# Two cross-attention layers on one core: layer 0's scores computed once and kept in SBUF, column maxima added back; turns of 128 queries, groups of four heads

## The chip, the core and the metric

One Trainium2 chip, of which the program uses one core. The metric is the time of one execution on the device in microseconds (us); the time before is 3849.66 us, the median of three runs (3845.82, 3850.59 and 3849.66). The profile is of one further execution, of 3851.3 us, whose instructions span 3849.6 us. Everything is float32.

## The reference: what is computed

Batch of 4, 512 queries of 320 channels, 1024 context rows of 512 channels, 20 heads of 16 channels. Two layers, one after the other, each with a residual:

```python
# layer 0 (x: 4 x 512 x 320, ctx: 4 x 1024 x 512; the last 4 context rows are "ip", the other 1020 "text")
probs_t  = softmax(q @ k_text.T * 0.25)              # per head: 512 x 1020
text_out = probs_t @ v_text                          # per head: 512 x 16
qsem     = l2norm(probs_t @ ctx_text)                # per head: 512 x 512, the costly product
fused    = q @ k_ip.T * 0.25 + 0.5 * qsem @ l2norm(ctx_ip).T
ip_out   = (softmax(fused) * spatial_mask) @ v_ip
x        = (text_out + ip_out) @ W_out + b_out + x
# layer 1 (the first 77 context rows are "text", the other 947 "ip")
x        = (softmax(q k_text) v_text + softmax(q k_ip) v_ip) @ Wo + bo + x
```

The product of every head's probabilities with the whole context (`qsem`) is needed only for its norm and its product with four vectors, but the norm needs all 512 channels, so each head multiplies 512 x 1020 by 1020 x 512.

## The kernel before

**Units of work.** A turn of layer 0 is a batch entry and a half `sh` of 256 queries; a group (`gi`, 80 in all) is one turn and a pair `p` of heads. A group has two `Head` units. A unit multiplies the exponentials `e` (in quarters: two 128-query halves by two halves of the context rows) by the context with a Strassen-like scheme of seven products (`part0` to `part3`, tiles `b`), each of four matmuls with 256 moving columns, or 277 where the 21 columns of this head's values (16 values, 4 products with the normalised ip rows, a one for the sum) are taken along through a window loaded by `window` (L709). POOL forms the sums of quarters (`sum2`, L754, L771, L774), DVE and ACT take the products out of PSUM, add and square them.

**Scores of layer 0, before: twice.** For each group and each `c` of four, `do_max` (L655) computes scores with queries on the partitions (`max_fill`, two matmuls of 512 columns, 16 rows deep, tile `mx`), and DVE takes the row maximum from PSUM (L663). `subtract_max` (L462) turns the maxima with two PE transposes (`pt_nm`) and puts them as extra rows under the queries (`qa`). `do_exp` (L671, `exp_fill` L448) computes the scores a second time with the context rows on the partitions (four matmuls of 256 columns, 19 rows deep, tile `ex`), so that the maximum is subtracted inside the matmul, and ACT exponentiates from PSUM into SBUF (L459). The 16 or 19 rows of a head lie in one of four 32-row groups of PE's array; a pair of heads uses two of them, and the next pair the other two.

**Layer 1** (`layer1_half`, L485) does the same, its scores twice, with two softmaxes over 77 and 947 rows, and multiplies by values 32 columns wide (`do_pv`, L520, tile `pv`, four heads in four 32-column groups). Its work lies in the queue `l1` and is taken out one step at a time.

**What sets the order.** PE executes in program order. Between the parts of a unit stand stops: `stop_a` (L924) takes one item from the queues (a moved maximum, a piece of the end of a turn, a step of the next batch entry's projections), then does `do_max` of group `gi + 2` and `do_exp` of `gi + 1`; `stop_b` (L939) takes an item and one step of layer 1. Other engines' instructions are placed by a scheduler near that order; each engine then runs its own list in order, and SP issues nearly all DMAs in its list's order. PSUM: two score tiles of two banks (`ps_sc`, tag `sc`), three banks for the products (`qs0` to `qs2`), one (`tp`) for everything else.

**Before and behind the loop.** Batch entry 0 is projected ahead of the loop, both layers' keys and values (L893 to L897), then the first two groups' scores. After the last group, layer 1 of the last 256 queries has nothing beside it.

In `queries` (L237) and the output projections (L566, L872) the 320 channels are contracted in chunks of 128, 128 and 64 rows.

Of the kernel before, what the change touches and what calls it, by code (L numbers as in the profile page):

```python
# [20 lines left out]
P = 128  # L21
# [3 lines left out]
NIP = 4  # L25
# [8 lines left out]
SH = S // 2  # L34
NP = H // 2
QT = 256


R_TXT, R_IP, R_ALL, KR = 16, 17, 18, 19
V0W = D + NIP + 1  # L40
# [6 lines left out]
NEVER = -1e30  # L47
ATTN_SCALE = 0.25
# [5 lines left out]
def xattn_pair(ctx_stack: ExitStack, tc: tile.TileContext, a: dict, out: bass.AP):  # L54
# [8 lines left out]
    ep = pool("ep", 8)  # L63
    st2 = pool("st2", 2)
# [13 lines left out]

    idle = [True]
# [23 lines left out]
    qq = [[cst.tile([P, SH], F32, name=f"qq{l}_{i}") for i in range(1 + l)] for l in range(2)]  # L103
    nmz = [[cst.tile([P, 2, P], F32, name=f"nmz{l}_{i}") for i in range(1 + l)] for l in range(2)]
# [6 lines left out]
    last = cst.tile([P, 2], F32, name="last")  # L111
    wq = [cst.tile([P, NC, C], F32, name=f"wq{i}") for i in range(2)]
# [9 lines left out]
    def load_x(b, sh, pl, tag):  # L122
        t = pl.tile([P, 2, C], F32, tag=tag, name=f"{tag}_{b}_{sh}")
        nc.sync.dma_start(t, a["x"][b, sh * SH : (sh + 1) * SH, :].rearrange("(t p) c -> p t c", p=P))
        return t
# [3 lines left out]
    def load_w(b, *names):  # L129
# [11 lines left out]
        if names == ("L0_xattn_W_v",):  # L141
# [4 lines left out]

    load_chunks(wq[0], "L0_xattn_W_q")
    nc.scalar.dma_start(bo[0], a["L0_xattn_b_out"].partition_broadcast(P))


    rows0 = st3.tile([2, T], F32, tag="e1", name="rows0")
    nc.gpsimd.memset(rows0, 1.0)
    nc.gpsimd.affine_select(out=rows0[:, 0:NTXT0], in_=rows0[:, 0:NTXT0], compare_op=ALU.not_equal, fill=0.0, base=-1,
                            pattern=[[0, NTXT0]], channel_multiplier=1)

    rows = st3.tile([3, T], F32, tag="e1", name="rows")
    nc.gpsimd.memset(rows, 1.0)
    nc.gpsimd.affine_select(out=rows[:, 0:NTXT1], in_=rows[:, 0:NTXT1], compare_op=ALU.not_equal, fill=0.0, base=-1,
                            pattern=[[0, NTXT1]], channel_multiplier=1)
    nc.gpsimd.affine_select(out=rows[:, NTXT1:T], in_=rows[:, NTXT1:T], compare_op=ALU.not_equal, fill=0.0, base=0,  # L160
                            pattern=[[0, T - NTXT1]], channel_multiplier=1)
    for l in range(2):
        for i in range(1 + l):
            nc.vector.memset(qq[l][i], 0.0)
            nc.vector.memset(nmz[l][i], 0.0)
            for r in range(4):
                if l:
                    nc.scalar.dma_start(kq[l][i][32 * r + R_TXT : 32 * r + KR, :], rows)
                else:
                    nc.scalar.dma_start(kq[l][i][32 * r + R_ALL : 32 * r + KR, :], rows0[0:1, :])  # L170
                    nc.scalar.dma_start(kq[l][i][32 * r + R_IP : 32 * r + R_ALL, :], rows0[1:2, :])
                    nc.scalar.dma_start(kq[l][i][32 * r + R_TXT : 32 * r + R_IP, :], rows0[1:2, :])
    nc.vector.memset(nmz[0][0].rearrange("p j (r n) -> p (j r) n", r=4)[:, :, R_IP], NEVER)
# [3 lines left out]
                            pattern=[[0, 2]], channel_multiplier=-1)  # L177
    for n in ("21", "t4"):
        nc.gpsimd.memset(xv[n], 0.0)
# [38 lines left out]
    def transposed_half(src, name, tag):  # L218

        t = big.tile([P, NC, SH], F32, tag=tag, name=name)  # L220

        def front():
            pt = tp(f"pt_{name}_a")
            for c in range(2):
                for j in range(2):
                    tr(pt[:, c * SH + j * P : c * SH + (j + 1) * P], src[:, j, c * P : (c + 1) * P], ident)
            evac(t[:, 0:2, :].rearrange("p c s -> p (c s)"), pt)

        def back():
            pt = tp(f"pt_{name}_b")  # L230
            for j in range(2):
                tr(pt[:64, j * P : (j + 1) * P], src[:, j, 2 * P : C], ident)
            evac(t[:64, 2, :], pt[:64, 0:SH])

        return t, [front, back]

    def queries(t, w, dst, name, tag):  # L237

        o = (st2 if tag == "kst" else big).tile([P, NC, SH], F32, tag=tag, name=f"qs_{name}")

        def front():
            pt = tp(f"pt_{name}_a")
            for c in range(2):
                for i, (_, n) in enumerate(CK):
                    mm(pt[:, c * SH : (c + 1) * SH], w[:n, i, c * P : (c + 1) * P], t[:n, i, :], i == 0, i == NC - 1)
            nc.vector.tensor_scalar(o[:, 0:2, :].rearrange("p c s -> p (c s)"), pt, ATTN_SCALE, None, ALU.mult)

        def back():
            pt = tp(f"pt_{name}_b")
            for i, (_, n) in enumerate(CK):  # L250
                mm(pt[:64, 0:SH], w[:n, i, 2 * P : C], t[:n, i, :], i == 0, i == NC - 1)
            nc.vector.tensor_scalar(o[:64, 2, :], pt[:64, 0:SH], ATTN_SCALE, None, ALU.mult)
            nc.sync.dma_start(dst[0 : 2 * P, :].rearrange("(c p) s -> p c s", p=P), o[:, 0:2, :])
            nc.sync.dma_start(dst[2 * P : C, :], o[:64, 2, :])

        return [front, back]

    def projections(b):
# [5 lines left out]
        z.qd = [[dr.tile([C, SH], F32, tag=f"q{l}_{sh}", name=f"qd{l}_{b}_{sh}") for sh in range(2)] for l in range(2)]  # L264
# [4 lines left out]
        def quarter(n):  # L269
# [4 lines left out]
            def buffer(tag, shape):  # L274

                return (big if b else ep).tile(shape, F32, tag=tag if b else "e0", name=f"{tag}_{b}_{n}")
# [118 lines left out]
            if n == 0:  # L395
                v1[0:1] = [lambda: values1_first(0), lambda: values1_first(1)]
            return [[lambda: turn(0), lambda: (turn(1), sums())], [lambda: keys(0)], [lambda: keys(1)], [last_keys],
                    [lambda: values0(0), lambda: values0(1)], v1, [values_ip] if n == 3 else []]

        quarters = [quarter(n) for n in range(4)]  # L400

        for kinds in quarters if b else zip(*quarters):
            for kind in kinds:
                steps += kind
        for sh in range(2):
            hold = {}

            def first(sh=sh, hold=hold):
                t, hold["x"] = transposed_half(load_x(b, sh, big, "xin"), f"xT0_{b}_{sh}", "raw")
                hold["q"] = queries(t, wq[0], z.qd[0][sh], f"q0_{b}_{sh}", "kst")  # L410
                hold["x"][0]()

            steps += [first, lambda hold=hold: hold["x"][1](), lambda hold=hold: hold["q"][0](),
                      lambda hold=hold: hold["q"][1]()]
        return z, steps


    def pair(p):
        return p // 2, 2 * (p % 2)

    def place(l, turn, p):


        g, r0 = pair(p)
        return buffer(l, turn, g), r0
# [4 lines left out]
    def load_pair(l, z, turn, g, i):  # L430
        k = buffer(l, turn, g)
        for r in range(2 * i, 2 * i + 2):
            c = 64 * g + 16 * r
            nc.sync.dma_start(qq[l][k][32 * r : 32 * r + D, :], z.qd[l][turn % 2][c : c + D, :])
            nc.sync.dma_start(kq[l][k][32 * r : 32 * r + D, :], z.kd[l][c : c + D, :])

    def max_fill(l, turn, p, c, name):

        k, r0 = place(l, turn, p)
        j, half = c // 2, c % 2  # L440
        ps = ps_sc.tile([P, 2, 512], F32, tag="sc", name=f"mx{name}_{c}")
        for i in range(2):
            r = 32 * (r0 + i)
            mm(ps[:, i, :], qq[l][k][r : r + D, j * P : (j + 1) * P],
               kq[l][k][r : r + D, half * 512 : half * 512 + 512], True, True)
        return ps

    def exp_fill(l, turn, p, c, qa, name):  # L448

        k, r0 = place(l, turn, p)  # L450
        ps = ps_sc.tile([P, 2, 512], F32, tag="sc", name=f"ex{name}_{c}")
        for j in range(2):
            for i in range(2):
                r = 32 * (r0 + i)
                t = (2 * c + j) * P
                mm(ps[:, i, j * SH : (j + 1) * SH], kq[l][k][r : r + KR, t : t + P], qa[r : r + KR, :], True, True)
        pl = st3 if l else ep
        e = pl.tile([P, 2, 2, SH], F32, tag=f"e{l}", name=f"e{name}_{c}")
        nc.scalar.activation(e.rearrange("p i j s -> p (i j s)"), ps.rearrange("p i n -> p (i n)"), AF.Exp)  # L459
        return e  # L460

    def subtract_max(l, turn, p, z, name):  # L462

        k, r0 = place(l, turn, p)
        pt = tp(f"pt_nm{name}")
        for j in range(2):
            tr(pt[:, j * P : (j + 1) * P], z[:, j, :], ident)
        lo = 32 * r0
# [4 lines left out]
    def nm_at(z, j, p, row):  # L473

        lo = 32 * (2 * (p % 2))
        return z[:, j, lo : lo + 64].rearrange("p (i n) -> p i n", i=2)[:, :, row]
# [537 lines left out]
```

## Time and profile before

| | |
|---|---|
| median of 3 runs | 3849.66 us |
| profiled execution | 3851.3 us (span 3849.6 us) |
| PE, matmuls | 3710.9 us busy, 96% of the span, 21972 records |
| PE, weight loads | 2633.4 us, 68% |
| DVE / ACT / POOL | 42% / 31% / 27% |
| first to last product `b` (the loop) | 196.1 to 3624.4 us |
| scores `ex` / `mx`, both layers | 759.0 us / 732.1 us of PE |
| DMA | 196.11 MB, most from SP's queue |

A line of the profile names the source line, the engine, the operation, the tile written and the tiles read with their shapes, and the number of records. A float32 matmul leaves two records, so that `ex ... x8` is four matmuls. "Busy" of PE is the union of records, whose ends are modelled: the distance between the starts of records says more than their lengths. The granted clock (PEclk) is 1.00 where PE has its full clock.

### The profile page before, as it was taken

How to read it: one execution, taken by the hardware profiler on the slowest of the kernel's cores; microseconds unless marked ns; L12 is line 12 of the kernel's file. 1: busy time of each engine (PE TensorE's matmuls, PEld its weight loads, DVE VectorE, ACT ScalarE, POOL GpSimd, SP SyncE). 2: the span in 40 equal slices, each digit the busy share in tenths (PEclk: the TensorE clock that was granted, in tenths of full speed). 3: DMA queues.
4: the chain of work that ended last, by engine and by line, in shares of the span. 5: the costliest groups of instructions: out<-in, count | busy, mean ns of one | idle time of the engine just before them, and what ended most of it. 6: DMA issues, size and time to landing. Idle time of an engine off the chain costs nothing.

```text
span 3849.6 us, 57354 instructions
## 1 busy us (share of the span) xinstructions
PE 3710.9 (96%) x21972; PEld 2633.4 (68%) x21972; DVE 1622.4 (42%) x3089; ACT 1195.9 (31%) x2424; POOL 1033.4 (27%) x1376
## 2 busy tenths in 40 slices
PE   5899999999999999999999999999999999999887
PEld 4577777677776777767776777767776676766533
DVE  1222234444434445344543545334544445355343
ACT  0122223233322333323332333323333333233222
POOL 1032233233322222223322222223332332322100
PEclk9899999999999999999999999999999999999955
DMA  6424411111232231211223232211211111111100
GB/s 178 121 67 109 108 41 17 18 28 23 59 74 64 66 89 37 53 37 28 67 52 76 62 74 48 53 34 28 61 22 31 29 22 26 30 21 25 24 19 13
DMA packets 541488, 196.11 MB, mean 51 GB/s; under 512 B 428056, under 2 KB 530936, under 8 KB 541216
## 3 DMA queue, kind: packets, MB, share of 16 engines
q1 hardware_dynamic: 540608, 192.10, 22.0%
q8 instruction: 175, 2.87, 0.3%
q14 instruction: 97, 0.79, 0.1%
q10 hardware_dynamic: 608, 0.35, 0.0%
HBM read 149.39 MB, written 40.16 MB: 49 GB/s over the span
## 4 chain that ended last, share of the span: by engine, by line
PE 91%; DVE 4%; DMA 3%; issue 1%; SPq 0%; ACT 0%; POOL 0%; POOLq 0%; DVEq 0%; ACTq 0%
PE b L74 53%; PE mx L74 11%; PE ex L74 9%; PE pv L74 5%; PE pt_k L74 4%; PE pt_v L74 4%; PE pt_y L74 2%; PE pt_q_a L74 1%; DVE den L550 1%; DVE m L506 1%; PE pt_nm L77 1%; DMA v1d<-v 1%; DMA raw<-in_ctx_dram 1%; PE pt_q_b L74 1%; DVE den L547 0%
## 5 line engine op out<-in xcount | busy, mean ns | idle before, releaser
L459 ACT ACTIVATE e<-ex 128x1024 f32<-128x1024 f32 x640 | 654.7, 1023 | 658.6 <-PE ex L74 655.6
L74 PE MATMUL ex<-qa,kq 19*128 19x256 f32 x5120 | 759.0, 417 | 10.1 <-DVE qa L517 7.3
L74 PE MATMUL mx<-kq,qq 16*128 16x512 f32 x2560 | 732.1, 673 | 28.1 <-DVE m L506 20.2
L74 PE MATMUL b<-xv_t,e 128*128 128x277 f32 x2560 | 674.2, 406 | 6.2 <-DVE c L762 6.0
L74 PE MATMUL b<-xv,e 128*128 128x277 f32 x2560 | 639.7, 402 | 0.5 <-DVE qa L470 0.5
L74 PEld LDWEIGHTS b<-xv_t,e 128*128 128x128 f32 x2560 | 471.5, 190 | 169.5 <-issue 54.0
L74 PEld LDWEIGHTS b<-xv,e 128*128 128x128 f32 x2560 | 473.8, 190 | 151.4 <-issue 44.8
L74 PEld LDWEIGHTS ex<-qa,kq 19*128 19x128 f32 x5120 | 454.9, 192 | 79.7 <-issue 16.7
L663 DVE TENSOR_REDUCE m<-mx 128x2 f32<-128x1024 f32 x320 | 390.0, 1219 | 222.5 <-PE ex L74 215.7
L758 ACT ACTIVATE junk<-c 128x256 f32<-128x256 f32 x480 | 200.2, 417 | 879.1 <-DVE c L762 879.0
L754 POOL TENSOR_TENSOR s<-e,e 128x256 f32<-128x256 f32 x320 | 228.6, 725 | 796.7 <-ACT e L459 648.3
L506 DVE TENSOR_REDUCE m<-mx 128x2 f32<-128x870 f32 (+1 forms) x320 | 364.4, 1139 | 170.1 <-PE ex L74 152.5
L675 POOL TENSOR_TENSOR e<-e 128x512 f32<-128x512 f32 x160 | 204.6, 1279 | 785.4 <-ACT e L459 776.7
L762 DVE TENSOR_TENSOR c<-b,p 128x256 f32<-128x256 f32 x320 | 134.1, 419 | 611.6 <-PE b L74 568.6
L74 PEld LDWEIGHTS mx<-kq,qq 16*128 16x128 f32 x2560 | 195.8, 191 | 246.6 <-issue 185.8
L74 PE MATMUL b<-xs,e 128*128 128x256 f32 x1280 | 318.6, 392 | 3.6 <-DVE p L782 3.6
L74 PE MATMUL b<-xs_t,e 128*128 128x256 f32 x1280 | 319.4, 392 | 1.4 <-POOL e L771 1.4
L771 POOL TENSOR_TENSOR e<-e,s 128x256 f32<-128x256 f32 x320 | 232.4, 728 | 325.9 <-PE b L74 325.9
L74 PE MATMUL b<-xs_t,s 128*128 128x256 f32 x1280 | 307.5, 383 | 0.0
L74 PEld LDWEIGHTS b<-xs,e 128*128 128x128 f32 x1280 | 233.5, 191 | 81.9 <-issue 41.6
L74 PEld LDWEIGHTS b<-xs_t,e 128*128 128x128 f32 x1280 | 229.9, 189 | 79.6 <-issue 26.2
L74 PEld LDWEIGHTS b<-xs_t,s 128*128 128x128 f32 x1280 | 241.7, 191 | 47.4 <-issue 15.6
(190 smaller groups left out, 2907.8 us busy)
## 6 DMA issues: line engine op xcount, KB each, us to landing
kq<-kd SPq DMA_DIRECT2D x320, 64.0 KB
v1q<-v1d SPq DMA_DIRECT2D x40, 373.5 KB
xv<-v0d SPq DMA_DIRECT2D x320, 42.0 KB
xv_t<-v0d SPq DMA_DIRECT2D x320, 42.0 KB
L_xattn_W_k<-in_L_xattn_W_k_dram SPq DMA_DIRECT2D x13, 640.0 KB
L_xattn_W_v<-in_L_xattn_W_v_dram SPq DMA_DIRECT2D x13, 640.0 KB
raw<-in_ctx_dram SPq DMA_DIRECT2D x32, 256.0 KB
td<-sums SPq DMA_DIRECT2D x64, 128.0 KB
```

The costliest lines, as they stand in the source:

```text
L74: tc.keep_in_program_order(nc.tensor.matmul(out, lhsT=lhsT, rhs=rhs, start=start, stop=stop, skip_group_check=on))
L77: tc.keep_in_program_order(nc.tensor.transpose(out, in_, ident))
L459: nc.scalar.activation(e.rearrange("p i j s -> p (i j s)"), ps.rearrange("p i n -> p (i n)"), AF.Exp)
L506: nc.vector.tensor_reduce(m[:, half, :], ps[:, :, 0 if half else NTXT1 : 512], AX.X, ALU.max, negate=True)
L550: nc.vector.reciprocal(d[:, k * SH : (k + 1) * SH], d[:, k * SH : (k + 1) * SH])
L663: nc.vector.tensor_reduce(ms[gi][:, j, half, :], ps[:, :, 0:n], AX.X, ALU.max, negate=True)
L675: nc.gpsimd.tensor_tensor(e[:, :, :, P:SH], e[:, :, :, P:SH], e[:, :, :, 0:P], ALU.subtract)
L754: nc.gpsimd.tensor_tensor(self.s2[:, 2 * k : 2 * k + 2, :], self.e("21", k), self.e("22", k), ALU.add)
L758: nc.scalar.activation(junk, x, AF.Square, accum_out=self.w["ss"][:, j, self.h, k : k + 1])
L762: nc.vector.tensor_tensor(c, x, y, ALU.add)
L771: nc.gpsimd.tensor_tensor(self.e("11", k), self.e("11", k), self.s2[:, 2 * k : 2 * k + 2, :], ALU.add)
```

## The change

Layer 0: a turn is now 128 queries, a group four heads of a turn (again 80 groups), a `Unit` two heads; the quarters of the seven products are two heads by two halves of the context rows. The scores are computed once, context rows on the partitions, 128 query columns per matmul, four heads in the four row groups (`fill`). ACT copies them from PSUM to SBUF, DVE takes maxima over the row tiles from PSUM, then `max0` turns the remaining 128 rows with four PE transposes, takes the column maxima, writes them to DRAM and reads them back spread over all partitions (`bc`). DVE and POOL add them in SBUF in place, and ACT exponentiates in place. `ew` holds these steps until three stops after `max0`.

Layer 1 still computes its scores twice, in turns of 128 queries; its steps are 20 per turn, linked from one turn to the next. Chunks of 64 rows are filled up with zeros to 128. Batch entry 0's keys and values of layer 1 are projected in the loop. There is a window of two heads' values (298 columns) in the first product.

```diff
-    def max_fill(l, turn, p, c, name):
...
+    def fill(c, m, name):
+        ps = [ps_sc.tile([P, 2, 512], F32, tag="sc", name=f"sc{name}_{c}_{i}") for i in range(2)]
+        for j in range(TH):
+            t = (TH * c + j) * P
+            for r in range(4):
+                mm(ps[r // 2][:, r % 2, j * P : (j + 1) * P], kq[0][0][32 * r : 32 * r + D, t : t + P],
+                   qq[0][0][32 * r : 32 * r + D, :], True, True)
+        e = []
+        for i in range(2):
+            e.append(ep.tile([P, 2, TH, P], F32, tag="e0", name=f"e{name}_{c}_{i}"))
+            nc.scalar.copy(e[i].rearrange("p h t s -> p (h t s)"), ps[i].rearrange("p h n -> p (h n)"))
+            nc.vector.tensor_reduce(m[:, c, 2 * i : 2 * i + 2, :],
+                                    ps[i][:, :, 0 : (TH - c) * P].rearrange("p h (t s) -> p h s t", s=P), AX.X, ALU.max)
+        return e
...
+    def fill0(gi, c):
...
+        if c:
+            m = ms[gi]
+            nc.vector.tensor_tensor(m[:, 0], m[:, 0], m[:, 1], ALU.max)
+            for i in range(2):
+                x = m[:, 0, 2 * i : 2 * i + 2, :]
+                nc.vector.scalar_tensor_tensor(x, x, drop[:, 0:1], e[i][:, :, TH - 1, :], ALU.add, ALU.max)
+            if gi + 1 < len(G):
+                turn, g = G[gi + 1]
+                load_quad(0, zs[TURNS[turn][0]], turn, g)
...
+    def max0(gi):
...
+        pt = tp(f"mx{name}").rearrange("p (h t) -> p h t", h=4)
+        for h in range(4):
+            tr(pt[:, h, :], m[:, 0, h, :], ident)
+        nc.vector.tensor_reduce(zz[:, 0:4], pt[:, :, 0 : P - NIP], AX.X, ALU.max, negate=True)
+        nc.vector.tensor_copy(of(turn)["ips"][:, 4 * g : 4 * g + 4, :], pt[:, :, P - NIP :])
+        zt = st2.tile([P, ZW], F32, tag="zt", name=f"zt{name}")
+        nc.vector.transpose(zt, zz)
+        zd = dr.tile([4, P], F32, tag="zd", name=f"zd{name}")
+        for k in range(P // ZW):
+            nc.sync.dma_start(zd[:, ZW * k : ZW * (k + 1)], zt[ZW * k : ZW * k + 4, :])
+        bc = big.tile([P, 4, P], F32, tag="bc0", name=f"bc{name}")
+        nc.sync.dma_start(bc, zd.partition_broadcast(P))
+
+        def do_exp(i, c):
+            e, mine = es[gi, i, c], bc[:, 2 * i : 2 * i + 2, :]
+            if c == 0:
+                nc.vector.tensor_tensor(e, e, mine.unsqueeze(2).to_broadcast([P, 2, TH, P]), ALU.add)
+            else:
+                nc.vector.scalar_tensor_tensor(e[:, :, TH - 1, :], e[:, :, TH - 1, :], drop[:, 0:1], mine, ALU.add, ALU.add)
+                (nc.gpsimd if i else nc.vector).tensor_tensor(
+                    e[:, :, 0 : TH - 1, :], e[:, :, 0 : TH - 1, :], mine.unsqueeze(2).to_broadcast([P, 2, TH - 1, P]), ALU.add)
+            flat = e.rearrange("p h t s -> p (h t s)")
+            nc.scalar.activation(flat, flat, AF.Exp)
+            if c == 0:
+                nc.gpsimd.tensor_tensor(e[:, 1], e[:, 1], e[:, 0], ALU.subtract)
+
+        later(3, [lambda i=i, c=c: do_exp(i, c) for i in range(2) for c in range(2)])
...
+        def do_exp(g, i, half):
...
+            for j in range(TH):
+                t = (TH * half + j) * P
+                for h in range(2):
+                    r = 32 * (2 * i + h)
+                    mm(ps[:, h, j * P : (j + 1) * P], kq[1][k][r : r + KR, t : t + P], qas[g][r : r + KR, :], True, True)
...
+    def stop(gi, k):
+        item()
+        if k == 3:
+            max0(gi + 1)
+        if k < 2:
+            fill0(gi + 1, k)
+        if k in (2, 4, 5, 6) or ending[0] and k < 2 or gi >= len(G) - HG and k == 7:
+            l1_step()
+        end_stop()
...
+    def end_stop():
+        stops[0] += 1
+        for _ in range(2):
+            if ew and ew[0][0] <= stops[0]:
+                ew.popleft()[1]()
...
+        for i in range(2):
+            u = units.pop((gi, i))
+            for k, part in enumerate((u.part0, u.part1, u.part2, u.part3)):
+                part()
+                stop(gi, 4 * i + k)
+                if k == 2:
+                    ahead(gi + i, 1 - i)
```

`ahead` makes the next unit and its `sum2`; `item` takes one entry from the queues of turned maxima, of a turn's end, or of projections; `l1_step` takes one step of layer 1. In a step, layer 1's maxima of the next group and the exponentials of this one are filled beside each other, as before; `do_pv` now takes all eight row tiles of a group in one go.

## The prediction

> **What bounds the kernel.** I read first the busy shares and the chain that ended last, then stretches of the span, then PE's timeline record by record.
>
> ```profile
> PE 3710.9 (96%) x21972; PEld 2633.4 (68%) x21972; DVE 1622.4 (42%) x3089; ACT 1195.9 (31%) x2424; POOL 1033.4 (27%) x1376
> PE 91%; DVE 4%; DMA 3%; issue 1%; SPq 0%; ACT 0%; POOL 0%; POOLq 0%; DVEq 0%; ACTq 0%
> ```
>
> PE is the bound, and the other engines are under half busy. Cut at the first and the last product `b`, the span falls into three stretches (us, then busy us of PE, weight loads, DVE, ACT, POOL, granted clock, DMA):
>
> ```profile
> 0.00:196.10 196.10, 132.45 (x504) 93.98 (x504) 35.79 (x79) 20.58 (x34) 24.42 (x64) 0.87 0.50 147
> 196.10:3624.40 3428.30, 3404.00 (x20521) 2457.07 (x20522) 1487.79 (x2850) 1126.80 (x2337) 995.46 (x1299) 1.00 0.22 48
> 3624.40:3849.60 225.20, 174.43 (x948) 82.38 (x946) 98.79 (x160) 48.57 (x53) 13.47 (x13) 0.59 0.07 19
> ```
>
> The loop leaves PE 24 us idle in 3428; so in it only PE's work counts. The two ends, 421 us, are a mixture of waits and, behind the loop, a clock of 0.59. Now PE's timeline (start, length):
>
> ```profile
> 533.24 2.03 PE L74 MATMUL b<-xv_t,e 128*128 128x277 f32 x8
> 535.20 0.70 PE L74 MATMUL mx<-kq,qq 16*128 16x512 f32 x2
> 535.21 0.70 PE L74 MATMUL ex<-qa,kq 19*128 19x256 f32 x4
> 535.73 0.59 PE L74 MATMUL mx<-kq,qq 16*128 16x512 f32 x2
> 535.75 0.60 PE L74 MATMUL ex<-qa,kq 19*128 19x256 f32 x4
> 536.27 2.13 PE L74 MATMUL b<-xv_t,e 128*128 128x277 f32 x8
> ...
> 2005.47 1.13 PE L74 MATMUL ex<-qa,kq 19*128 19x256 f32 x8
> 2006.53 1.07 PE L74 MATMUL pv<-e,v1q 128*32 128x256 f32 x16
> ...
> 2018.21 0.60 PE L77 MATMUL pt_xT_a<-ident,xr 128*128 128x128 f32 x4
> ```
>
> The reader is to see that `mx` and `ex` together hold PE from 535.20 to 536.27, 1.07 us, and `ex` alone from 2005.47 to 2006.53, 1.06 us. They use different row groups and run side by side: **the second computation of the scores is already free.** With 0.09 us ahead and 0.10 us in the first record behind (where the array changes between row groups and the whole), a visit costs 1.26 us.
>
> **The change, part by part (against the 3849.6 us span).** *Scores of layer 0.* Before, a group makes four visits; two groups' worth of records fill four row groups. After, `fill` also fills all four, with half the columns: two visits per group. Each row group gets 4 matmuls, 8 records of 128 columns; at the 0.109 us between the starts of the transposes (four in 0.60 us, the last 0.27 long) that is 0.87, with the same edges 1.26 us. 160 visits less: -202 us.
>
> [...] `ex` alone, eight records in two row groups, four after each other in each, takes 1.06 us, which is 4 x 0.216 and an edge[...]. I take 0.109.
>
> *Other PE work in the loop.* Four transposes per group for two: 160 x 0.109 = +17. The two-head window: 1280 records 21 columns longer, at (0.233 - 0.216)/21 us each: +22. `pv` in one visit per 128 queries, instead of four per 256: two edges of 0.24 us fewer, 37 times, so with small change -15. Zero-filled chunks: a 64-row chunk now costs 0.39 us of edges (in `pt_q_a` its records stand 0.31, 0.32, 0.31 and 0.32 us apart where 0.216 is usual); 68 of them in the loop, less eight new 64-column visits: -23. Layer 1's keys and values of batch entry 0 come into the loop: 18.2 us of `pt_k` and 21.7 of `pt_v` at the clock of 0.83 to 0.91 there, +35. Four fewer layer 1 visits: -5. Layer 1's records of 128 columns cost nothing more, as above. PE's sum: -171 us.
>
> *What is added elsewhere.* ACT: 320 copies of 1024, like the exponentials 1.02 us, +327 us, 45% busy. DVE per group: before, four maxima of 1.22 and small ones, 6.7 us; after, two PSUM maxima of 1024 (1.22) and two of 768 (0.95), one SBUF maximum of 512 (0.69), four of 256 (0.42), one of 496 (0.68), adds of 1024 (1.22, twice) and 768, small ones: 11.2 us. +360 us, 56% busy. (Lengths by 0.15 us + 1.04 ns per element, from 0.42 at 256 and 1.22 at 1024. That the maxima read with a stride no row shows beyond 160 elements in fours, 0.32 us, the plain price; [...] at twice the price 4.4 us per group would come on.) POOL: 80 sums of 768, 1.8 us from 0.73 at 256 and 1.28 at 512. Averages hide all this. What they don't hide are three waits in a group of some 36 us.
>
> (1) Both score tiles are filled at once, and in DVE's list each maximum follows ACT's copy. The second tile is free some 3.9 us after a fill; only 3.45 us of products lie between the two fills. 0.5 us, unless an item stands there: 30 us in all.
>
> (2) The maxima's way. Count from the end of a group's first `part0`. By adding up PE's list, `part3` ends at 15.2 (3.45 + 1.26 + 3.6 + 1.26 + 2.2 + 1.87, waits included). The transposes follow, DVE has the shuffle and reciprocal of layer 1 ahead (0.4 + 1.73), so `zt` is ready at 17.6. SP issues four writes (0.42 each), then must wait until they land. The nearest row is `qd` and `qq` behind the loop: issued at 3655.53, the read's issue at 3657.67, 2.1 us. `bc` is issued at 21 and lands, 256 KB, after 3 to 4.5 us: 24 to 25.5. PE, if nothing waits, is by then at `part1` of the second unit, and needs at 30.4 that DVE has done `c` (L783) for its `part3`, and at 27 that ACT has copied `u`. But DVE's list puts 4.2 us of adds and a maximum of 1.22 ahead of that `c`, and the copy of `u` stands behind one or two exponentials that wait for these adds. Without collisions `c` is done at 30.7 to 32. With them it is later:
>
> ```profile
> 1282.22 1.29 POOL L675 TENSOR_TENSOR e<-e 128x512 f32<-128x512 f32 x1 [8.11 <-ACT e L459]
> 1282.48 1.32 DVE L300 TENSOR_TENSOR sums<-raw 128x256 f32<-128x256 f32 x1
> ...
> 2067.95 0.43 DVE L300 TENSOR_TENSOR sums<-raw 128x256 f32<-128x256 f32 x1 [1.36 <-POOL e L675]
> ```
>
> The same DVE add takes 0.43 us alone and 1.32 where it starts beside POOL, ending with it and 0.3 us more. [...] Added at the row's lone price the wait is 0.3 to 2 us[...]. I take 3 us in the 24 groups with no item to cover it, 1.5 in the 32 with pieces of a turn's end, 0.3 in the 24 with projections (each item some 2 us): 127 us. Ends: 0 and 250.
>
> (3) 16 turn ends of 20 small DVE operations instead of 8, ahead of the first fill's maxima: 1.3 us each, 20 us.
>
> Together 177; the loop's idle time before, 24, mostly goes: net +155. Loop: 3428 - 171 + 155 = 3412.
>
> *Ahead of the loop.*
>
> ```profile
> 46.94 2.82 PE L77 MATMUL pt_cT<-ident,raw 128*128 128x128 f32 x12 [21.68 <-ACT cT L95]
> ```
>
> PE waits 21.7 us for ACT, which issues 20 small DMAs for constant rows; these go, and the raw loads (which then set it) can end near 25. Layer 1's `pt_k` and `pt_v` (42 us with their waits) go too. But the round trip of `bc` comes with nothing beside it, some 13 us. 196 - 20 - 42 - 20 (eight `mx` and four `ex` visits, for two fills) + 13 gives 127; I take 125 (112 to 145).
>
> *Behind it.* 225 us become a turn of 128 queries: finish, one piece, queries, `qd` round trip 27; first maxima 6; 20 steps at the 2.85 us that a step takes there, 57; five `pv` 20; the last normalisation and output, half as long, 14: 124 (115 to 135). Steps of one chain take this long whatever is before them, so nothing hides here.
>
> **Sum.** 125 + 3412 + 124 = 3661 us, with the 1.7 us outside the span 3663; the median stands 1.6 under the profiled execution. Forecast 3660 us, the loop nearly unchanged, the ends 172 shorter.
>
> **Rivals.** *1. The waits are covered:* [...] `bc` comes early, net 0: 3505 us. For it: PE's loop has been patient so far (24 us idle). Against: (2) has no slack. *2. The waits are longer, but not decisive:* net 250 to 330, 3755 to 3835. *3. Slower, by weight loads:* [...] it decides from 0.158 us per record (the forecast's gain of 188 us over 3840 records is 0.049, on 0.109). The `ex` row speaks against it. *4. Slower, by the wait for `bc`:* DVE's list stands at the first add, behind it `c`, behind that PE's `part3`. Each us later per group is 80 us; from 4.3 us net per group (gains of 171 + 172 over 80) it decides. If waits over 3 us also bring the clock down, as behind the loop (0.59), it goes faster: 5 us and 2 us of half clock give 4060. For it: SP is in order, and windows and key loads stand between `zd` and `bc`. That the change doesn't do what it says: only one visit in four row groups counts, so if `fill`'s groups run two by two, each visit is 2.1 us and the loop 138 longer, in rival 2's range.
>
> **Chances.** Forecast's own range, 3570 to 3750: 0.53. Rival 1: 0.13. Rival 2: 0.17. Rival 3: 0.03. Rival 4: 0.14. A measurement tells 0.2% from no change: faster 0.82, same 0.02, slower 0.16. The range 3510 to 3850 leaves out about 0.2.
>
> **What would show it.** Right: 160 `sc` visits of 1.26 us (64 records within 1.1 us); `qs` products unchanged; first product near 125 us; 124 us behind the last; in groups without items a PE gap of 2 to 4 us before the last product of the second unit, put down to DVE `c` or ACT `u`, DVE's adds longer than 1.22 us beside POOL. Wrong: `sc` records 0.2 us apart; no such gap; a granted clock under 0.95 in the loop.

## The result, and the profile after

The changed kernel takes 4208.3 us (median of 4 runs, 4195.89 to 4217.77) against 3849.72: 1.0932 times the time before (95% interval 1.09 to 1.0963). Forecast were 3660 us and a range to 3850. The profiled execution took 4212.84 us, its span is 4211.1.

The page's busy shares and the chain that ended last, after:

```profile
PE 3723.9 (88%) x28996; PEld 2931.6 (70%) x28996; DVE 2219.7 (53%) x3716; ACT 1514.9 (36%) x2824; POOL 1246.6 (30%) x1134
PE 63%; DVE 18%; DMA 10%; SPq 3%; ACT 3%; issue 2%; POOL 0%; DVEq 0%; POOLq 0%; ACTq 0%
```

PE was 91% of the chain; now DVE, DMA and SP's queue hold 31% of it. No engine is full; DVE's 53% says nothing of who waits for whom. Cut as before, at the first and the last product `b` (us, then busy us of PE, weight loads, DVE, ACT, POOL, granted clock, DMA):

```profile
0.00:109.52 109.52, 72.44 (x353) 56.33 (x353) 31.28 (x65) 17.74 (x29) 21.50 (x55) 0.90 0.66 189
109.52:4079.68 3970.16, 3565.09 (x27624) 2808.72 (x27625) 2137.61 (x3558) 1466.72 (x2757) 1215.73 (x1064) 0.93 0.27 60
4079.68:4211.12 131.44, 86.42 (x1021) 66.54 (x1019) 50.85 (x94) 30.46 (x38) 9.39 (x16) 0.67 0.12 31
```

The ends came near the forecast: 109.5 us (125) and 131.4 (124), together 180 shorter than before. The loop didn't: 3970 us where 3412 were forecast and 3428 stood. In it PE is idle for 405 us (24 before), and PE's busy time is 3565 (3404 before, 3233 forecast) at a granted clock of 0.93. What PE and DVE waited for (total us, times, longest):

```profile
PE b L77 <- DVE p L804: 212.5, 63, 7.0
PE mx L77 <- DVE m L496: 31.3, 30, 3.0
PE ex L77 <- ACT e L518: 27.5, 26, 1.7
...
DVE e L693 <- DMA bc<-zd: 328.3, 80, 8.5
```

More than half of the idle time ends with L804, the copy of `p5` (`part1`), an instruction that the change didn't touch. One group of the timeline shows why (start, length, engine; in brackets the idle time ahead):

```profile
3266.10 0.21 DVE L683 STREAM_TRANSPOSE zt<-zz 128x32 f32<-128x32 f32 x1
...
3266.87 2.41 SPq L549 DMA_DIRECT2D oT<-oq  x4
...
3269.38 1.43 SPq L686 DMA_DIRECT2D zd<-zt  x4
...
3270.91 1.48 SPq L738 DMA_DIRECT2D xv<-v0d  x3
...
3271.88 1.89 PE L77 MATMUL b<-xs_t,s 128*128 128x256 f32 x8
3272.58 0.36 SPq L688 DMA_DIRECT2D bc<-zd  x1
...
3275.91 1.23 DVE L693 TENSOR_TENSOR e<-e,bc 128x1024 f32<-128x1024 f32 x1 [4.50 <-DMA bc<-zd]
3275.96 2.85 POOL L696 TENSOR_TENSOR e<-e,bc 128x768 f32<-128x768 f32 x1 [5.59 <-DMA bc<-zd]
3277.05 0.42 DVE L804 COPY p<-b 128x256 f32<-128x256 f32 x1
...
3277.39 1.70 DVE L695 SCALAR_TENSOR_TENSOR e<-e,drop,bc 128x256 f32<-128x256 f32 x1
...
3277.62 3.75 PE L77 MATMUL b<-xs,e 128*128 128x256 f32 x8 [2.74 <-DVE p L804]
```

Read it from the top. The maxima are ready (`zt`) at 3266.31. SP first issues four writes of layer 1's `oT`: it waits 0.56 us until POOL has made `oq`, and the four issues take 2.41 us. So the writes of `zd` start 3.07 us late. `bc` is issued at 3272.58 and has landed by 3275.9, when the first additions start. DVE has stood at its first addition for 4.5 us by then; the copy `p5` is behind it, and PE, which wanted to start its next product at 3274.88, stands for 2.74 us. Then that product takes 3.75 us and its successor starts 3.54 us after it (3281.16); where nothing waits it starts after 1.83. The granted clock (the value behind POOL's) of this product, and of the stretch behind the next one, says why:

```profile
3277.62:3281.37 3.75, 3.75 (x9) 3.03 (x10) 3.75 (x3) 1.18 (x3) 2.59 (x2) 0.50 0.00 0
...
3285.00:3288.40 3.40, 3.40 (x30) 2.54 (x29) 2.42 (x5) 2.80 (x6) 1.47 (x2) 1.00 0.32 77
```

PE has half its clock behind the wait: 2.74 us of waiting have cost another 1.7 us in this one product.

### The profile page after: what moved, and what is told of

Its sections match the earlier page's. It is cut to its first block, busy times and chain, and to the rows that moved or that the text cites. A ratio compares the mean times of both kernels' runs of the same rounds, so it can differ in the third digit from the quotient of the medians.

```text
span 4211.1 us, 74174 instructions
## 1 busy us (share of the span) xinstructions
PE 3723.9 (88%) x28996; PEld 2931.6 (70%) x28996; DVE 2219.7 (53%) x3716; ACT 1514.9 (36%) x2824; POOL 1246.6 (30%) x1134
## 4 chain that ended last, share of the span: by engine, by line
PE 63%; DVE 18%; DMA 10%; SPq 3%; ACT 3%; issue 2%; POOL 0%; DVEq 0%; POOLq 0%; ACTq 0%
PE b L77 39%; DMA bc<-zd 7%; PE pv L77 5%; PE ex L77 4%; PE sc L77 4%; DVE e L695 4%; DVE e L693 4%; PE pt_k L77 3%; DVE e L696 3%; PE pt_v L77 2%; PE mx L77 2%; DVE m L463 2%; PE pt_q L77 2%; DVE m L496 1%; SPq L738 1%
## 5 line engine op out<-in xcount | busy, mean ns | idle before, releaser
L77 PE MATMUL b<-xv,e 128*128 128x277 f32 (+1 forms) x2560 | 658.0, 410 | 12.0 <-ACT e L699 12.0
L77 PE MATMUL b<-xs,e 128*128 128x256 f32 x1280 | 407.6, 474 | 212.5 <-DVE p L804 212.5
L699 ACT ACTIVATE e<-e 128x1024 f32<-128x1024 f32 x320 | 337.6, 1057 | 695.9 <-DVE e L693 456.3
L463 DVE TENSOR_REDUCE m<-sc 128x256 f32<-128x1024 f32 (+1 forms) x320 | 338.1, 1088 | 285.8 <-ACT e L462 285.8
L77 PE MATMUL mx<-kq,qq 16*128 16x512 f32 x1280 | 393.2, 688 | 85.0 <-DVE m L496 31.3
L77 PE MATMUL ex<-qa,kq 19*128 19x128 f32 x5120 | 404.9, 301 | 47.4 <-ACT e L518 27.5
L518 ACT ACTIVATE e<-ex 128x1024 f32<-128x1024 f32 x320 | 325.2, 1017 | 222.3 <-PE ex L77 221.8
L794 POOL TENSOR_TENSOR e<-e,s 128x512 f32<-128x512 f32 x160 | 202.8, 1267 | 632.0 <-PE b L77 632.0
L693 DVE TENSOR_TENSOR e<-e,bc 128x1024 f32<-128x1024 f32 x160 | 208.6, 1304 | 328.3 <-DMA bc<-zd 328.3
L462 ACT COPY e<-sc 128x1024 f32<-128x1024 f32 x320 | 308.0, 1014 | 173.1 <-PE sc L77 171.4
L696 POOL TENSOR_TENSOR e<-e,bc 128x768 f32<-128x768 f32 x80 | 225.4, 2818 | 457.5 <-DMA bc<-zd 449.0
```

The lines of the kernel that those rows point to most:

```text
L77: tc.keep_in_program_order(nc.tensor.matmul(out, lhsT=lhsT, rhs=rhs, start=start, stop=stop, skip_group_check=on))
L462: nc.scalar.copy(e[i].rearrange("p h t s -> p (h t s)"), ps[i].rearrange("p h n -> p (h n)"))
L463: nc.vector.tensor_reduce(m[:, c, 2 * i : 2 * i + 2, :], ps[i][:, :, 0 : (TH - c) * P].rearrange("p h (t s) -> p h s t", s=P), AX.X, ALU.max)
L693: nc.vector.tensor_tensor(e, e, mine.unsqueeze(2).to_broadcast([P, 2, TH, P]), ALU.add)
L696: (nc.gpsimd if i else nc.vector).tensor_tensor(e[:, :, 0 : TH - 1, :], e[:, :, 0 : TH - 1, :], mine.unsqueeze(2).to_broadcast([P, 2, TH - ...
L699: nc.scalar.activation(flat, flat, AF.Exp)
```

## Experiments

In the median over the 80 groups of the changed kernel, 3.1 us pass from `zt` to the first write of `zd`, 1.1 from the first to the last of the four writes, 2.1 to the issue of `bc` and 3.6 until an addition starts: 9.6 us from end to end. **Theory:** PE's own work is as forecast; DVE stands still until `bc` lands, PE behind it, and half clock follows each wait. **Rivals:** DVE's 600 us more of work, or its collisions with POOL, make the loop longer by themselves; or only the copy `p5` is in the wrong place.

### 1. Maxima that are there early

```diff
+        bc = big.tile([P, 4, P], F32, tag="bc0", name=f"bc{name}")
+        nc.sync.dma_start(bc, old.partition_broadcast(P))   # zd of the group before
         pt = tp(f"mx{name}").rearrange("p (h t) -> p h t", h=4)
...
-        nc.sync.dma_start(bc, zd.partition_broadcast(P))
```

> The changed kernel, with one thing altered: a group's `bc` is read from the maxima of the group before it, and the read is issued at the head of max0 instead of behind the writes of `zd`. The maxima are still found and written, and DVE and POOL make the same additions; what is left out is that a group subtracts its own maxima. Theory (PE waits because DVE stands at the first addition until `bc` lands, 5.5 us per group with the half clock behind the wait): of the loop's 405 us of idle time some 300 go and of the 320 us at the lower clock some 250, so 3650 us (3560 to 3760), granted clock in the loop 0.98 or more. Rival (the loop is longer because DVE has 600 us more to do [...]): the additions are the same, so it stays above 4100 us.

Measured: 3888.5 us, ratio to before 1.01 (1.0077 to 1.0123). With the same additions 320 us are gone and the waits for L804's counterpart nearly so (12 us). The loop:

```profile
110.35:3751.59 3641.24, 3409.41 (x27624) 2703.07 (x27625) 1908.18 (x3558) 1460.61 (x2757) 1096.75 (x1064) 0.97 0.29 65
```

So the number of DVE's additions is not what costs the time. But it is far from 3650: the loop is still 232 us idle, in many smaller waits elsewhere (34 us of the transposes for ACT's copy `pc`, 32 us of `pv` for a turn's end); DVE's order has changed too. The run also took the collisions of DVE with POOL away (the rows under 5): in 2 groups only, not in 80, do DVE's and POOL's additions start together. So by itself it does not part the wait for `bc` from the collisions; the runs under 4 and 5 do.

### 2. Only the copy ahead of the additions

```diff
         def do_exp(i, c):
+            if p5_copy[0] is None:
+                adds(i, c)
+            else:
+                with tc.issue_after(p5_copy[0].ins):     # on DVE's list, behind the last p5
+                    adds(i, c)
+
+        def adds(i, c):
             e, mine = es[gi, i, c], bc[:, 2 * i : 2 * i + 2, :]
...
-            nc.vector.tensor_copy(self.p5, self.b3)
+            p5_copy[0] = nc.vector.tensor_copy(self.p5, self.b3)
```

> The changed kernel with the additions of `bc` queued on DVE behind the copy `p5` of the second unit, nothing else. Theory (it is the copy `p5` behind the first addition for which PE waits): the 212 us in front of the product of `xs` and `e` go, with the lower clock behind them (some 150 us); part of it comes back ahead of the last product of the unit, since the sum `c` now stands behind all the additions: 3900 us (3800 to 4000). If DVE's amount of work is the cause, the wait only moves: 4150 to 4230.

Measured: 4148.96 us (ratio 1.0781, 1.0765 to 1.0797). The theory's number was missed; the time is at the edge of the rival's: the wait moved. PE's waits in this run:

```profile
PE mx L77 <- DVE m L496: 114.0, 56, 4.3
PE b L77 <- ACT u L816: 88.7, 43, 3.9
...
PE b L77 <- DVE c L792: 23.2, 37, 3.5
PE b L77 <- DVE p L813: 22.7, 7, 4.8
```

`p5` fell from 212 to 23 us, but layer 1's maxima, the sum `c` and ACT's copy `u` (behind exponentials that wait for the additions) are late instead. What stands behind the additions is late while `bc` is. Whether the late landing or the amount of DVE's work is to blame, this run does not say; the first run under 4 does.

### 3. The price of a wait

Fill the hole with useless products:

```diff
             self.product(self.b1[:, self.c1], "s2", "t2", False)
+            if self.i:
+                fill = tp(f"fill_{self.name}")
+                for t in range(TH * 2):
+                    mm(fill[:, 0:EH], ident, xs["22"][:, t % TH, :], t == 0, t == TH * 2 - 1)
```

> The changed kernel with eight more records of 256 columns (1.75 us) on PE at the place of the wait, ahead of the product of `xs` in each second unit; their result is not used. Theory (a wait of 2.5 us or more also brings the half clock for some 4 us): the records fill the wait (108 of their 140 us) and keep it under 2 us, so the product behind it takes 1.83 us again in place of 2 to 3.6: 4090 us (4030 to 4150). If the clock doesn't follow from the wait, the records cost their 32 us: 4240 us (4220 to 4330).

Measured: 4185.43 us (1.0886, 1.0853 to 1.0918). It fits neither number. I had mis-sized the filler: eight matmuls are 16 records, 3.55 us, not 1.75. With the true size it can be read:

```profile
107.99:4053.26 3945.27, 3744.41 (x28904) 2969.03 (x28905) 2134.00 (x3558) 1467.54 (x2757) 1214.94 (x1064) 0.96 0.27 60
```

284 us of useless work (80 x 3.55) made the loop 25 us shorter. Idle time fell by 204 (405 to 201), and PE's other work by 105 (3565 + 284 - 3744), at a clock of 0.96 for 0.93. If only the idle time had changed, the loop would have been 80 us longer (284 less 204).

The other way round, on the kernel before the change: make DVE late by repeating the copy of `p5`.

```diff
-            nc.vector.tensor_copy(self.p5, self.b3)
+            for _ in range(14 if self.i else 1):         # 7 in the second run
+                nc.vector.tensor_copy(self.p5, self.b3)
```

> The kernel before the change, with the copy `p5` of the second head of each group made 14 times in a row (13 more DVE copies of 0.42 us), so that PE must wait some 2.9 us per group for DVE, with DVE still under 60% busy. If a wait costs only itself: 80 x 2.9 = 232 us more, 4080 us. Theory (half clock behind each wait, another 2 us): 4240 us (4170 to 4310), with a granted clock of 0.94 to 0.96 in the loop.

> The kernel before the change with the copy `p5` of each second head made 7 times (14 times gave waits of 3.9 us, the loop 313 us idle and 145 us more at the lower clock). Seven copies fewer are 2.9 us, so waits of 1.0 us, 80 us in all. If the lower clock comes in proportion to the wait, 3968 us; if a wait of this length brings none, 3930 us (3915 to 3945).

Measured: 4311.25 us (1.1202, 1.1185 to 1.1218) and 3894.96 us (1.0111, 1.0094 to 1.0128). The loop with 14 copies, then with 7, each with PE's wait for the copy:

```profile
196.03:4081.86 3885.83, 3548.73 (x20521) 2550.78 (x20522) 1901.02 (x3890) 1127.78 (x2337) 995.83 (x1299) 0.95 0.19 42
PE b L74 <- DVE p L783: 294.7, 77, 7.6
```

```profile
195.22:3669.62 3474.40, 3411.41 (x20521) 2459.64 (x20522) 1683.78 (x3330) 1126.08 (x2337) 993.49 (x1299) 0.99 0.22 47
PE b L74 <- DVE p L783: 36.8, 33, 4.9
```

PE executes the same 20521 records as in the loop before (3404.0 us busy). With waits of 3.8 us on average it is 313 us more idle and 145 us longer busy: a wait of this length costs 1.46 times itself (458 us for 313). With waits of 1.1 us it is 39 us more idle and 7 us longer busy. My two numbers were both low for 14 copies (the waits are longer than the 2.9 us I expected), and both high for 7, where only 33 groups waited for this copy at all.

### 4. `bc` early on SP

```diff
+        if k == 3:
+            max0(gi + 1)
         item()
-        if k == 3:
-            max0(gi + 1)
...
-        nc.sync.dma_start(bc, zd.partition_broadcast(P))
+        last_bc[0] = nc.sync.dma_start(bc, zd.partition_broadcast(P)).ins
...
+    def dma(o, i):            # for the DMAs named in each run
+        ins = nc.sync.dma_start(o, i)
+        if last_bc[0] is not None:
+            tc.add_manual_dep(ins.ins, last_bc[0].name,
+                              mybir.DependencyInfo(mybir.DependencyClass.NoSync, mybir.DependencyReason.DATA),
+                              reason="behind bc")
+        return ins
```

The first lines put the four transposes of `max0` ahead of their stop's item. First all of SP's DMAs behind `bc`, with the additions as in run 2:

> The changed kernel with the additions behind the copy `p5` (as in the run before of that kind), and in SP's list `zd` and `bc` ahead of layer 1's four writes of `oT` and of all loads that the program names behind them, so that `bc` lands some 3 us earlier in each group. Nothing else differs from that run, which took 4149 us. If the wait for `bc` is the cause, DVE's 226 us in front of the first addition go and with them the lower clock: 3900 us (3830 to 4000). If the additions and exponentials themselves are (their amount, or their collisions), it stays at 4080 to 4150.

Measured: 3882.77 us (1.008, 1.0065 to 1.0095), 266 less than run 2, with the same additions at the same place of DVE's list. Something else differs from run 2 after all, the place of the transposes; more of that below. New: PE waits 158 us ahead of pieces of the projections and of turn ends (tiles `pt_`; 17 in the changed kernel), 137 of them for weights and context that are now loaded behind `bc`, up to 11 us at a time. So the same with only `oT` and the windows behind `bc`:

> As the run with `bc` early and the additions behind the copy, but only `oT`'s writes and the windows stand behind `bc` on SP; the loads of weights and context are left where the changed kernel has them (in the earlier run PE waited some 130 us more for those, up to 11 us at a time). If these waits are what was left, 3650 us (3600 to 3720); if the additions are, over 3780.

Measured: **3711.41 us, 0.9642 of the time before (0.9626 to 0.9657)**, at the upper end of the expectation. The loop, and the same place in a group:

```profile
107.23:3582.08 3474.85, 3352.65 (x27624) 2675.64 (x27625) 2008.14 (x3558) 1457.57 (x2757) 1185.93 (x1064) 0.98 0.30 68
```

```profile
3118.98 0.21 DVE L694 STREAM_TRANSPOSE zt<-zz 128x32 f32<-128x32 f32 x1
3119.22 1.27 SPq L697 DMA_DIRECT2D zd<-zt  x4
...
3121.43 0.35 SPq L699 DMA_DIRECT2D bc<-zd  x1
...
3121.87 2.41 SPq L96 DMA_DIRECT2D oT<-oq  x4
...
3124.96 0.42 DVE L822 COPY p<-b 128x256 f32<-128x256 f32 x1 [0.67 <-PE b L77]
3125.30 2.43 DVE L711 TENSOR_TENSOR e<-e,bc 128x1024 f32<-128x1024 f32 x1
...
3127.68 1.99 PE L77 MATMUL b<-xs,e 128*128 128x256 f32 x8
```

`bc` is issued 2.2 us after `zt` (6.3 in the changed kernel), has landed before DVE has copied `p5`, and the product of `xs` follows without a wait at full clock. From `zt` to the first addition 5.7 us pass in the median over the groups (9.6 in the changed kernel). PE executes exactly the records of the changed kernel: 283 us less idle (405 to 122) and 212 us less busy (3565 to 3353). These 495 us are all but 2 of the difference, and they came from order alone: that of SP's and DVE's lists, and of the four transposes, which go ahead of their stop's item. That last change was not made by itself. In the 18 groups without other work no item stands there, and in them too the idle time falls, from 4.3 us to 0.75 (4.0 in run 2); how much the transposes' place gives in the other groups stays open.

Is the queue enough, with DVE's order left to the scheduler?

> The changed kernel with `bc` early on SP (ahead of `oT`'s writes and the windows), and DVE's order left to the scheduler, which then puts three or four additions ahead of the copy `p5` in 68 groups (23 in the changed kernel). If only the time at which `bc` lands matters, the wait goes: under 3900 us. If what counts is how much stands ahead of the copy when `bc` lands (three additions with their collisions, 4.7 us), PE still waits some 3 us per group: 4130 us (4050 to 4230).

Measured: 3900.9 us (1.0128, 1.011 to 1.0145), at the first theory's edge and far from the second's 4130. PE's wait for the copy:

```profile
PE b L77 <- DVE p L813: 107.9, 55, 3.1
```

I put this wait at 3 us in every group; it is 2 us or more in some 35. So of 497 us SP's order, with the transposes' place, gives 307, and the copy's place, which alone gave 59, another 189: each gives more with the other.

### 5. Collisions, and other places for the additions

```diff
-                (nc.gpsimd if i else nc.vector).tensor_tensor(
+                nc.vector.tensor_tensor(
```

> The changed kernel with POOL's addition of 768 elements given to DVE; the wait for `bc` is untouched. If DVE's slowness beside POOL makes the loop longer (the addition of 768 takes 2.01 us beside POOL's in place of 0.96, the one of 256 ahead of it 1.50 in place of 0.48), some 2 us per group with the lower clock behind, 240 us, go: under 4000 us. If it is the wait for `bc`, only those groups gain in which the copy `p5` stands behind three additions (about a third): 4130 us (4080 to 4200).

Measured: 4107.58 us (1.0662, 1.0647 to 1.0678): 100 us less than the changed kernel, within the range for the wait for `bc` and not under 4000, the number for the collisions. It takes only one collision away, that with POOL's addition. The collisions are real; DVE's small and middle addition, in the changed kernel and then in run 1 (busy us, mean ns):

```profile
L695 DVE SCALAR_TENSOR_TENSOR e<-e,drop,bc 128x256 f32<-128x256 f32 x160 | 219.9, 1374 | 0.0
L696 DVE TENSOR_TENSOR e<-e,bc 128x768 f32<-128x768 f32 x80 | 147.3, 1841 | 0.0
```

```profile
L703 DVE TENSOR_TENSOR e<-e,bc 128x768 f32<-128x768 f32 x80 | 76.7, 958 | 0.0
L702 DVE SCALAR_TENSOR_TENSOR e<-e,drop,bc 128x256 f32<-128x256 f32 x160 | 71.0, 479 | 0.0
```

Collisions make the first of these rows nearly three times as long and the second twice. POOL's addition starts within 0.2 us of one of DVE's in all 80 groups, since one event releases both, the landing of `bc`; 78 of DVE's additions of 256 run beside it. The addition of 768 never does: it runs beside POOL's next work, the subtraction in `e` (L701), which I had taken for its addition. In run 1, 77 of the 80 additions of 768 have nothing of POOL's beside them. But the collisions don't decide: in the run of 3711 us POOL's addition still runs beside DVE's first one in 48 of 80 groups (2.43 us for it in the lines under 4), and it is 497 us faster.

Last, the second unit's additions later than the first's, to relieve the end of a group. With all of SP's DMAs behind `bc`, with the loads free, and with both additions inside the group:

```diff
-        later(3, [lambda i=i, c=c: do_exp(i, c) for i in range(2) for c in range(2)])
+        later(3, [lambda c=c: do_exp(0, c) for c in range(2)])
+        later(5, [lambda: do_exp(1, 0)])
+        later(6, [lambda: do_exp(1, 1)])            # 5 in the last run
...
+            with tc.issue_after(last_dve() if i else p5_copy[0].ins) if p5_copy[0] is not None else nullcontext():
+                adds(i, c)
```

`last_dve()` is DVE's last instruction so far: the second unit's additions are held behind it in these three runs.

> As the run with `bc` early and the additions behind the copy, and besides the second unit's two additions and exponentials are done at the end of the group and at the start of the next one, not together with the first unit's. Theory (PE's work is what was forecast, all else is waits for this one step and the clock behind them): idle time in the loop under 120 us, granted clock 0.98, 3600 us (3540 to 3700). If other waits come in their place (score tiles not free, the first maxima late), 3700 to 3850.

> As the run in two steps, with only `oT`'s writes and the windows behind `bc` on SP. Groups without other work took 36.0 us there, all of it PE's work; 3896 less the 130 us of waits for loads and some 90 us of lower clock behind them: 3650 us (3590 to 3710). If the waits for DVE's maxima of `sc` (41 us there) weigh more than what is saved at the end of a group, it is slower than the run with all four additions together.

> As the two-step run with the loads left free (3726 us), but both additions of the second unit stand at the end of the group, none in the next group. In that run PE waited 42 us for DVE's maxima of `sc` at 13 turn starts, with the lower clock behind, while its groups without other work took 36.0 us against 37.0 in the run with all four together (3711 us). If the addition at the start of the next group caused those waits, 3680 us (3650 to 3705); if a turn's own small operations do, it stays at 3715 to 3735.

Measured: 3899.4 us (1.0127, 1.0112 to 1.0142), 3726.24 (0.9682, 0.9666 to 0.9698) and 3756.75 (0.9753, 0.9738 to 0.9768). The first missed its 3600; PE waits for weights and context in it, as under 4 (156 us ahead of `pt_` tiles). The second missed its 3650 as well, and is its other case, slower than all four together; but it shows PE's bare work: a group without other work, from 2700.06 to 2736.10, takes 36.04 us with no idle time, where the same kind took 38.1 before. Yet PE waits 42 us in the loop for the maxima of `sc` (14.5 in the run of 3711 us), at the starts of turns: more than is gained elsewhere. The third falsified my reason for that: without an addition in the next group the wait is 55 us, and the time fits neither of my cases. Why is open; in DVE's list the additions then stand ahead of a turn's 20 small operations, but that wasn't tried by itself.

## Why the prediction was wrong, point by point

The loop took 558 us more than the 3412 forecast: 226 of them are idle time of PE (405 for 179), 332 its busy time (3565 for 3233), and 212 of these 332 went when only the order was changed.

- *PE's work in the loop, 171 us less:* right in kind, too high in size. A `sc` visit takes 1.30 us with its edges (forecast 1.26), 1.10 of them its own 32 records (the 64 in my last paragraph was a slip), and a group without other work 2.1 us less than before (forecast 2.2). Busy time without the waits for `bc` is 3353 us, not 3233: some 70 of the 120 are the clock of 0.98 over 3475 us, the rest I can't assign.
- *Weight loads don't count (rival 3):* right, 1.10 us per visit of 32 records in four row groups.
- *Both ends:* right in sum, 241 us against 249; the sum is closer than its parts (15.5 us too long and 7.4 too short), which is luck.
- *Waits (1) and (3), 50 us together:* both end at a score tile, and PE waited 15 us for those.
- **Wait (2), 127 us: here it failed.** PE waited 212.5 us for the copy `p5` alone, which the forecast did not name, and lost another 212 to the half clock, which it put at nothing. It went wrong in four places. (a) *"needs at 30.4 that DVE has done `c` ... and at 27 that ACT has copied `u`"*: PE needs another result first, that of the copy `p5`, which in DVE's list stands behind one addition in 43 groups and behind three or four in 23. In the group shown above PE wants it at 25.2 on the same count, and `bc` has landed at 26.2. (b) *"SP issues four writes"* as soon as `zt` is ready (17.6; in this group 16.6): four writes of `oT` are ahead, 3.1 us (0.56 of waiting for POOL, the rest their issue). The 2.1 us to the read's issue are as forecast, though three loads stand in them, and the 3.6 to the landing are too. (c) *"1.5 in the 32 with pieces of a turn's end, 0.3 in the 24 with projections"*: the items hide nothing. At this place PE waits 2.4 us on average in the 18 groups without other work, 2.9 in 37 with pieces of a turn's end and 2.4 in 25 with projections. (d) The clock was put into rival 4 alone: 212 us, nearly as much as the waits. The sign I had set for being wrong, a clock under 0.95 in the loop, came: 0.93.
- *Collisions:* by the means under 5 they cost DVE 2.7 us per group (2 x 0.90 and 0.88 us). What I had added for them (3 us taken for a group without an item, where the lone price gave 0.3 to 2) was my estimate, 1 to 2.7 us. They are not what decides.
- *Rival 4* is what happened, with its mechanism, its 5 us per group (405 us of idle time over 80) and the clock (212 over 80 is 2.7 us, where 2 were put). It had 0.14, and its 4060 us were 150 short: the sum of its own terms, 3505 + 80 x 7, is 4065; with the measured 7.7 it is 4121, and the remainder is the 120 us under the first point, less the 24 us of idle time that the loop had anyway and what the ends differ. The pick among the cases was the error: I had written that waits over 3 us might bring the clock down, and still priced waits of 3 us at 3 us.

The clock records of the 14 traces show when the lower clock came: half clock begins and ends on a fixed grid of 3.41 us. Of the steps of this grid at full clock in the loops, 436 of the 439 in which PE stood idle for 2 us or more were followed by a step at half clock; 98 of 196 with 1.5 to 2 us; 83 of 12886 with less than 1 us. Such a step need not be idle all through: in the changed kernel's loop 62 of 62 with 2 us or more were followed by half clock, and in only 8 of these was PE idle throughout. So waits of 2.7 us were not free: in the changed kernel half clock follows 79 of the 84 waits of 2.5 us or more. Below 1.5 us it comes less often: it follows 4 of the 31 waits of 1 to 1.5 us in the run of 3711 us, and 13 of the 30 steps with 1 to 1.5 us of idle time in the changed kernel's loop.

## What to carry to other kernels

When a change puts a transfer's landing in front of work on an in-order engine, list every instruction behind the waiting one, also those that the change didn't touch, and every DMA ahead of the transfer on its queue, and ask of each who waits for it. In these runs waits of PE of 3.8 us on average cost 1.46 times themselves (458 us for 313), so price a recurring wait with the clock behind it. And here a change that made the kernel 9% slower made it 3.6% faster with the same instructions in another order: look at the order before giving up the idea.

## What the runs showed of the hardware that was not expected

- Half clock after short waits: 3.8 us of waiting cost 1.8 us more, 1.1 us only 0.2 (7 us over 33 waits). By PE's idle time within one 3.41 us step of the clock record, half clock followed in 436 of 439 cases with 2 us or more and in 83 of 12886 with less than 1 us.
- PE work that is thrown away can pay: 284 us of it took 25 us off the loop.
- A read of what was just written to DRAM was issued 1.3 us (median, run of 3711 us) after the start of the last write's issue where nothing stood between, 2.1 us (changed kernel) with three loads between.
- Issuing takes time on SP's queue: four writes of `oT` took 2.41 us to issue, whether SP had just waited for POOL (3266.87) or not (3121.87).
- Additions of DVE and POOL that run beside each other take longer: DVE's of 256 elements 1.50 us (median) where 0.48 is usual, POOL's of 768 elements 2.85 for 1.84. DVE's of 768 elements took 2.01 us for 0.96 beside a subtraction of POOL's.
